# A four-layer graph attention kernel: mask gathers moved between layers, and the first edge blocks of layer 0 rearranged

## The chip, the core and the metric

The kernel runs on one core of a Trainium2 chip. The metric is the device time of one execution in microseconds. The core's engines are TensorE (PE, its weight loads PEld), VectorE (DVE), ScalarE (ACT), GpSimd (POOL) and SyncE (SP); indirect DMAs (gathers by a list of indices) are issued on POOL, most plain DMAs on SP. All waits between engines are semaphores placed by a tile framework from the program order: each engine executes its own instructions in the order in which the program issues them.

## What is computed

4096 nodes with 256 features each, an adjacency matrix of 4096 x 4096 int32, and four graph attention layers, each followed by a residual and a layer norm. Node degrees fall off along the index (the chance of an edge goes with the square root of 1/(i+1) and 1/(j+1)), so the matrix is dense in its first rows and columns and sparse elsewhere.

```python
def attention(logits, mask, h):            # in every layer, per head
    return softmax(where(mask, logits, -big), axis=1) @ h
# layer 0, 8 heads: leaky_relu(e_l[i] + e_r[j], 0.2) + gate * sum_f |c[i,f] - c[j,f]| * Wc[h,f]
# layer 1, 1 head:  s_src[i] + s_dst[j] + b_att,       h = x @ W_fc + b_fc
# layer 2, 4 heads: leaky_relu(s_row[i] + s_col[j], 0.2), elu, + x @ Wr + br, a layer norm of its own
# layer 3: h = x @ W0, then three attention layers (leaky_relu slope 0.01), each with elu
x = layernorm(x + layer0(x, adj)); x = layernorm(x + layer1(x, adj))
x = layernorm(x + layer2(x, adj)); x = layernorm(x + layer3(x, adj))
```

## The kernel before

**Two forms of sparsity.** Rows of the output are taken in 32 chunks of 128 in layer 0, and in 16 pairs of chunks (256 rows) in layers 1 to 3. Layer 0's chunk 0 is dense (`rows0`). Its other 31 chunks walk *edges*: for each row chunk a list of its edges is built, cut into 445 tiles of 128 edges and grouped in 64 blocks of 5 to 10 tiles. Layers 1 to 3 walk *nodes*: for each pair a list of the nodes with any edge into its 256 rows, in tiles of 128 nodes (`PAIR_TILES`: 32 tiles for pair 0, which is always dense, then 25, 22, 20, 19, 18, 17, 16, 16, 15, 15, 14, 14, 14, 13, 13, in all 251 for pairs 1 to 15). `DENSE = {1: 6, 2: 1, 3: 3}` says how many of the first pairs each later layer takes densely instead, all 32 node tiles with masks of their own: six in layer 1, so that layer 1 uses listed tiles of pairs 6 to 15 only (147), layer 2 those of pairs 1 to 15 (251), layer 3 those of pairs 3 to 15, three times. `sequence` interleaves a layer's dense and listed tiles; `LEAD[2] = 32` dense tiles go first in layer 2.

**Layer 0's start.** A projection of 32 node tiles fills V; every fourth tile the list builder `list_edges` is driven by six steps on DVE and ACT (L1153). Then V is multiplied by v tile by tile on DVE (L1175), and each tile is written to a table in DRAM (`table0`, L1177) on SP, 32 DMAs of 139 KB. `rows_by_edges` begins with constants: a memset of two `dT` tiles (L619), an iota on POOL (L707) and its casts to `number`, `count` and `place`.

**A block of edges** (`Block`, L621 to L702) goes through stages: `middle` (ACT: u), `spread` (DVE: of_row, then PE), `nodes` (DVE: the indices of the edges' nodes), `gather` (POOL: one indirect DMA from table0 for each tile, L659, into `g`, three buffers), `differences` (DVE: d, L666, PE, ACT), `pair_terms`, `weights`, `rows`, `values` (DVE multiplies g by w) and `add` (PE, L702, the last reader of g). The main loop is a software pipeline written out by hand: at block i it issues `spread` and `nodes` of block i+3, `gather` of block i+2, `differences` of block i+1, and the rest of block i. Between these steps `lane` lets other work run: the list builders of later chunks and of the pairs (DVE, ACT, PE), and two queues of mask jobs, one entry of each per edge tile.

**Mask jobs.** For each listed node tile of a pair the 128 x 256 adjacency cells are gathered by `listed_mask`: an indirect DMA on POOL into `pair_m` (L1020), a conversion to bytes on DVE (`pair_mb`, L1024) and a store to `listed_d` on SP (L1025). `job` issues the gather at once and the conversion seven entries later. `list_pair` puts the jobs of pairs 1 to 12 (`q < LATE`, 211 tiles) in the queue served in layer 0, those of pairs 13 to 15 (40) in `late_jobs`; `cell` is the tile of their indices. What is in the queue when the blocks end is drained there.

**Layers 1 to 3** run `attend` (L1266): for each tile of the sequence it issues the weights (for listed tiles a load of the mask on SP and an indirect gather of the node's row from the layer's table on POOL, L1312, 16 buffers; then DVE), the products of an earlier tile on PE, one step of `aside`, and one step of the ends of finished pairs (`one`: normalisation, the next layer's projection). In layer 1 `aside` is `late_masks()`: it issues one gather of `late_jobs` per tile and the conversion of the one five before. Layer 1 scales and writes its table on DVE and POOL first; in layer 2 ACT scales V and POOL issues four DMAs to table 2 (L1489); POOL also adds beta to the residual rows in `one` (L1527).

Of the kernel before, what the change touches and what calls it, by code (L numbers as in the profile page):

```python
# [49 lines left out]
F32 = mybir.dt.float32  # L50
# [3 lines left out]
U16 = mybir.dt.uint16  # L54
# [7 lines left out]
P = 128  # L62
# [11 lines left out]
DENSE = {1: 6, 2: 1, 3: 3}  # L74

LATE = 13
LEAD = {1: 80, 2: 32, 3: 44}
# [3 lines left out]
def gnn_stack(ctx: ExitStack, tc: tile.TileContext, a: dict, out: bass.AP):  # L81
# [365 lines left out]

    def rows0(chunks, ends, ps, ps_s, ps_acc):

        with ExitStack() as st:
            two = st.enter_context(tc.tile_pool(name="l0_all_two", bufs=2))
            three = st.enter_context(tc.tile_pool(name="l0_all_three", bufs=2))
            got = st.enter_context(tc.tile_pool(name="l0_all_got", bufs=3 * JR))
            cjs = []
# [142 lines left out]

    def rows_by_edges(prepared, pair_w, ends, ps, lane, first):  # L600

# [7 lines left out]
        with ExitStack() as st:  # L609
            two = st.enter_context(tc.tile_pool(name="l0_two", bufs=2))  # L610
            got = st.enter_context(tc.tile_pool(name="l0_got", bufs=3))
            ps_acc = st.enter_context(tc.tile_pool(name="l0_acc", bufs=2, space=PSUM))
            ps_x = st.enter_context(tc.tile_pool(name="l0_x", bufs=2, space=PSUM))
            number = two.tile([P, BT, P], U16, name="number", bufs=1)
            place = two.tile([P, max(EDGE_TILES)], F32, name="place", bufs=1)
            count = two.tile([P, P], F32, name="count", bufs=1)
            dTs = [two.tile([ROW1 + 1, P], F32, name=f"dT{k}", bufs=1) for k in range(2)]
            for d in dTs:
                nc.vector.memset(d[0:ROW1], 0.0)  # L619
                nc.vector.memset(d[ROW1:], 1.0)  # L620

# [81 lines left out]

            number_i = two.tile([P, BT * P], I32, name="number_i", tag="to_row")
            nc.gpsimd.iota(number_i, pattern=[[1, BT * P]], base=0, channel_multiplier=0)  # L707
            nc.vector.tensor_copy(number.rearrange("p t r -> p (t r)"), number_i)
            nc.vector.tensor_copy(count, number_i[:, 1:P + 1])
            place_i = two.tile([P, max(EDGE_TILES)], I32, name="place_i", bufs=1)  # L710
            nc.gpsimd.iota(place_i, pattern=[[P, max(EDGE_TILES)]], base=1, channel_multiplier=1)
            nc.vector.tensor_copy(place, place_i)

            plan = [Block(c, b, t0, n) for c in range(FIRST, NC) for b, (t0, n) in enumerate(blocks_of(c))]
# [5 lines left out]
            def at(i, *what):  # L720
                if 0 <= i < B:
                    for w in what:
                        getattr(plan[i], w)()

            dense = first(lambda shape, name: ps_x.tile(shape, F32, name=name, tag="x"),
                          lambda shape, name: ps_acc.tile(shape, F32, name=name, tag="acc0", bufs=1))
            given = 0
            for i in range(3):
                at(i, "middle", "spread", "nodes")
                if i < 2:  # L730
                    at(i, "gather")
            at(3, "middle")
            at(0, "differences", "pair_terms", "rows", "weights")
            late = []
            for i, blk in enumerate(plan):
# [7 lines left out]
                blk.values()  # L743
                at(i + 2, "gather")
                at(i + 1, "pair_terms")
                lane(share, c)
                at(i + 3, "nodes")
                lane(share, c)
# [21 lines left out]
    def layer0(proj):  # L770
        lin = 1.0 - 0.2
        with ExitStack() as st:
# [56 lines left out]
            nc.vector.memset(ones8, 1.0)  # L829
            near_by = [lp.tile([P, N + 8 * max(sum(k) for k in kinds)], BF16, name="near"), None]  # L830

            adj_pool = st.enter_context(tc.tile_pool(name="l0_adj", bufs=1))
# [140 lines left out]
            def list_pair(q):  # L973
# [3 lines left out]
                at = ats[q // BP]  # L977
                cell = lists.tile([P, A], I32, name="cell", bufs=LATE - 1) if q < LATE else keep.tile([P, A], I32, name=f"cell{q}")
                rhs = lists.tile([P, NT, 2, A], BF16, name="rhs", bufs=1)
# [30 lines left out]
                nc.vector.tensor_scalar(cell, x[:, 1], float(N // PW), float(q), ALU.mult, ALU.add)  # L1010
                if q < LATE:
                    jobs.extend([lambda i=i: listed_mask(at_pool, q, i, cell) for i in range(A)])
                else:
                    late_jobs.extend([lambda pool, i=i: listed_mask(pool, q, i, cell) for i in range(A)])
# [104 lines left out]
            with ExitStack() as pr:  # L1119
# [19 lines left out]
                for T in range(NT):  # L1139
# [13 lines left out]
                    if T % 4 == 3:  # L1153
                        for _ in range(6):
                            next(edge_lists)
# [4 lines left out]
                with tc.tile_pool(name="l0_st", bufs=1) as sp:  # L1160
# [13 lines left out]
                    for T in range(NT):  # L1174
                        nc.vector.tensor_tensor(by_head[:, T], by_head[:, T],  # L1175
                                                v[:, T, :].unsqueeze(2).to_broadcast([P, H0, D0 + 1]), ALU.mult)
                        nc.sync.dma_start(table0[T * P:(T + 1) * P, :], V[:, T, :])  # L1177

# [39 lines left out]
            def lane_e(n, c):  # L1218

                for _ in range(n):  # L1220
                    lane(1, (14 / EDGE_TILES[c], 5 / EDGE_TILES[c]))
                    ends.step()

            rows_by_edges(prepared, pair_w, ends, ps, lane_e,
                          lambda ps_s, ps_acc: rows0(FIRST, ends, ps, ps_s, ps_acc))
            proj.sums()
# [120 lines left out]
    def ends_of(ended, pairs, nxt, ps, one):  # L1347

        for _ in range(6):
            yield  # L1350
        if nxt is not None:
            yield from nxt.prepare(ps)
        for n in range(pairs):
            while not ended:
                yield
            yield from one(ended.pop(0), n)
# [7 lines left out]
    def layer1(proj, nxt, seq):  # L1364
        with ExitStack() as st:
# [50 lines left out]

            def late_masks():

                begun = []
                while late_jobs:  # L1420
                    begun.append(late_jobs.pop(0)(work))
                    if len(begun) > 4:
                        begun.pop(0)()
                    yield
                for convert in begun:
                    convert()

            def one(state, n):
# [15 lines left out]

            attend(seq, opened, weights, products, lambda ended: ends_of(ended, NP, nxt, ps, one), aside=late_masks())
            nxt.sums()
# [6 lines left out]
    def layer2(proj, V, nxt, seq):  # L1453
# [3 lines left out]
        with ExitStack() as st:  # L1457
# [54 lines left out]
            def products(some):  # L1512
# [4 lines left out]
                for (_, _, _, den, _), k, (g, w), last in some:  # L1517
                    for h in range(H2):
                        nc.tensor.matmul(den[32 * h:32 * h + 1, :], g[:, (h + 1) * (D2 + 1) - 1:(h + 1) * (D2 + 1)], w[:, h],  # L1519
                                         start=False, stop=last)  # L1520

            def one(state, n):
                q, _, num, den, _ = state
# [35 lines left out]

            attend(seq, opened, weights, products, lambda ended: ends_of(ended, NP, nxt, ps, one), rate=1.6, batch=2)  # L1560
            nxt.sums()
# [78 lines left out]
    def layers(p1, sparse):  # L1640

        def plan(n):
            k = DENSE[n] if sparse else NP
            return sequence(range(k), range(k, NP), LEAD[n])

# [28 lines left out]
    with tc.If(nc.values_load(over[0:1, 0:1], min_val=0, max_val=1) > 0):  # L1674
        with ExitStack() as st:
# [10 lines left out]
            for _ in rows0(NC, ends, ps, lambda shape, name: pool.tile(shape, F32, name=name, tag="s"),  # L1686
                           lambda shape, name: pool.tile(shape, F32, name=name, tag="acc0")):
                ends.step()
# [56 lines left out]
```

## Time and profile before

| | us |
|---|---|
| runs of the kernel before: median (lowest to highest) of 3 | 3169.53 (3165.16 to 3173.18) |
| the profiled execution: its time | 3159.55 |
| its span, first to last instruction | 3157.8 |
| mean granted TensorE clock in it | 0.881 of full speed |
| busy PE, PEld | 2574.0 (82%), 1798.6 (57%) |
| busy DVE, ACT, POOL | 2277.2 (72%), 1329.2 (42%), 1966.0 (62%) |
| layer 0: V multiplied from; table written; first gather | 104.6; 105.2 to 121.7; 135.3 |
| layer 0: gather 278 of 445; last gather | 747.0; 1149.7 |
| layer 1: first attention matmul | 1205.5 |
| layer 2: first weights; last tile | 1487.1; 2177.7 |
| layer 3: from; to the end | 2216; 3157.8 |

The page is taken from one execution of the program by the hardware profiler. Engines are busy when they execute an instruction; for POOL's indirect DMAs that is the time in which it makes their descriptors, not the time of the transfer. "Releaser" of an idle time is what ended it, inferred from semaphores. "issue" is time in which an engine waited for nothing that the profile shows. L12 is line 12 of the kernel before; a name such as g<-table says what an instruction writes and reads.

### The profile page before, as it was taken

The page shows a single profiled execution, that of the slowest core. Times are in us where ns is not written, and L with a number is a line of the kernel's source. Part 1 is how long each engine was busy: PE and PEld are TensorE (multiplying, and loading weights), DVE is VectorE, ACT ScalarE, POOL GpSimd, SP SyncE. Part 2 cuts the span into 40 slices and gives each one's busy share as a digit, 9 for nine tenths or more (in the row PEclk, how much of TensorE's full clock was granted, in tenths as well). Part 3 has the DMA queues.
Part 4 walks back from the last instruction along what each step waited for, and adds up shares of the span by engine and source line. Part 5 has one row for each costly group of instructions (what it writes and reads, how often), then busy time and mean ns, then how long its engine had stood idle before and what let it go on. Part 6 is the DMA issues. An engine that isn't in the chain of part 4 may idle for free.

```text
span 3157.8 us, 53737 instructions
## 1 busy us (share of the span) xinstructions
PE 2574.0 (82%) x16067; PEld 1798.6 (57%) x16067; DVE 2277.2 (72%) x7545; ACT 1329.2 (42%) x3895; POOL 1966.0 (62%) x1874
## 2 busy tenths in 40 slices
PE   6266666656666556998999999998899999999997
PEld 5154454444545445996233333333788878887875
DVE  6767888888888856776878788886565556556666
ACT  3365565646666434776212223333222322233334
POOL 0277667777777756772475566551477647755775
PEclk8587777777676778998999999999999999999999
DMA  6567786657666447675333333331544454446554
GB/s 183 164 195 224 234 249 190 206 169 220 198 217 204 115 128 233 200 206 155 105 89 101 96 104 99 100 86 51 171 137 135 114 174 135 135 113 183 166 164 129
DMA packets 345937, 495.65 MB, mean 157 GB/s; under 512 B 120476, under 2 KB 252418, under 8 KB 345634
## 3 DMA queue, kind: packets, MB, share of 16 engines
q0 software_dynamic: 87600, 252.16, 28.5%
q1 hardware_dynamic: 239608, 223.19, 23.6%
q10 hardware_dynamic: 18432, 16.79, 1.6%
q8 instruction: 132, 2.16, 0.3%
q14 instruction: 165, 1.35, 0.1%
HBM read 426.20 MB, written 65.72 MB: 156 GB/s over the span
## 4 chain that ended last, share of the span: by engine, by line
PE 51%; DMA 4%; DVE 2%; ACT 2%; issue 1%; POOL 0%; ACTq 0%; DVEq 0%; SPq 0%; POOLq 0%
PE acc L1605 20%; PE num L1515 12%; PE den L1519 8%; PE acc L1414 4%; PE ph L209 4%; DMA g<-table,pair_idx 3%; PE xT_p L198 1%; PE pr L213 1%; DVE w L1599 1%; PE pt L1537 0%; ACT V L1585 0%; POOL g L1312 0%; DVE y L1617 0%; DVE bn_st L305 0%; DVE y L314 0%
## 5 line engine op out<-in xcount | busy, mean ns | idle before, releaser
L1312 POOL DMA_INDIRECT g<-table,pair_idx x1010 | 1113.5, 1102 | 523.4 <-PE den L1519 102.6
L659 POOL DMA_INDIRECT g<-table,idx x445 | 515.5, 1158 | 194.0 <-issue 116.5
L1605 PE MATMUL acc<-g,w 128*128 128x257 f32 x2448 | 574.7, 382 | 17.3 <-DVE w L1599 16.7
L1605 PEld LDWEIGHTS acc<-g,w 128*128 128x128 f32 x2448 | 457.9, 190 | 94.7 <-DVE w L1599 30.0
L1506 DVE SCALAR_TENSOR_TENSOR w<-R,g,mask 128x256 f32<-128x256 f32 x1004 | 438.4, 486 | 48.2 <-PE den L1519 47.9
L1599 DVE SCALAR_TENSOR_TENSOR w<-R,g,mask 128x256 f32<-128x256 f32 x612 | 292.2, 482 | 244.8 <-PE acc L1605 172.8
L1515 PE MATMUL num<-w,g 128*64 128x256 f32 x2008 | 367.6, 395 | 0.0
L1020 POOL DMA_INDIRECT pair_m<-in_adjT,cell x251 | 279.2, 1112 | 112.4 <-issue 46.0
L702 PE MATMUL acc<-g,to_row 128*128 128x264 f32 x890 | 304.4, 502 | 41.3 <-DVE g L689 32.5
L1605 PE MATMUL acc<-V,w 128*128 128x257 f32 x1152 | 284.6, 387 | 16.1 <-ACT V L1585 9.1
L702 PEld LDWEIGHTS acc<-g,to_row 128*128 128x128 f32 x890 | 216.1, 255 | 95.1 <-DVE g L689 38.7
L1519 PE MATMUL den<-w,g 128*1 128x256 f32 x2008 | 266.5, 378 | 0.0
L1515 PEld LDWEIGHTS num<-w,g 128*64 128x64 f32 x2008 | 140.5, 135 | 196.9 <-DVE w L1506 97.4
L1605 PEld LDWEIGHTS acc<-V,w 128*128 128x128 f32 x1152 | 221.4, 194 | 49.7 <-ACT V L1585 15.0
L1615 ACT ACTIVATE y<-acc,inverse 128x256 f32<-128x256 f32 x96 | 44.7, 466 | 417.2 <-DVE inverse L320 365.9
L209 PE MATMUL ph<-wx,xT 128*128 128x258 f32 (+3 forms) x640 | 185.4, 423 | 33.4 <-ACT xT L200 19.7
L1599 DVE SCALAR_TENSOR_TENSOR w<-R,V,mask 128x256 f32<-128x256 f32 x288 | 137.0, 481 | 87.0 <-PE acc L1605 74.2
L905 DVE FIND_INDEX8 cand<-ones,near 128x8 uint16<-128x520 bf16 (+8 forms) x424 | 195.1, 469 | 0.0
L696 ACT ACTIVATE to_row<-count,side 128x128 f32<-128x128 f32 x445 | 145.4, 391 | 102.8 <-PE acc L702 99.5
L200 ACT ACTIVATE xT<-xT_p 128x128 f32<-128x128 f32 x320 | 86.0, 276 | 196.3 <-PE xT_p L198 187.2
L874 ACT ACTIVATE near<-ai 128x64 bf16<-128x64 int32 (+1 forms) x186 | 138.4, 765 | 59.4 <-DMA ai<-in_adj 31.2
L209 PEld LDWEIGHTS ph<-wx,xT 128*128 128x128 f32 x640 | 125.7, 206 | 64.8 <-ACT xT L200 31.4
(327 smaller groups left out, 4290.2 us busy)
## 6 DMA issues: line engine op xcount, KB each, us to landing
ai<-in_adj SPq DMA_DIRECT2D x124, 512.0 KB
mask<-listed_d SPq DMA_DIRECT2D x228, 128.0 KB
at<-in_adjT SPq DMA_DIRECT2D x96, 256.0 KB
mask<-mask_d SPq DMA_DIRECT2D x128, 128.0 KB
g<-table,pair_idx POOLq DMA_INDIRECT x1010
R<-r_d SPq DMA_DIRECT2D x56, 256.0 KB
table<-V POOLq DMA_DIRECT2D x12, 1032.0 KB
s<-y ACTq DMA_DIRECT2D x96, 128.0 KB
```

Of the source, the lines that this page charges most:

```text
L209: nc.tensor.matmul(ph, xT[:, kt, :], self.wx[:, kt, :], start=kt == 0, stop=kt == 1)
L659: nc.gpsimd.indirect_dma_start(self.g[:, t, :], None, table0[:, :], bass.IndirectOffsetOnAxis(ap=self.idx[:, t:t + 1], axis=0))
L696: nc.scalar.activation(self.to_row[:, t], count, AF.Abs, bias=self.side[:, t, 0:1])
L702: nc.tensor.matmul(acc, self.to_row[:, t], self.g[:, t, 0:VW], start=self.t0 + t == 0, stop=last and t == n - 1)
L905: nc.vector.max_index(cand[:, s], ones8, near[:, at:at + W])
L1020: nc.gpsimd.indirect_dma_start(m[:, :], None, pair_cells, bass.IndirectOffsetOnAxis(ap=cell[:, k:k + 1], axis=0))
L1312: nc.gpsimd.indirect_dma_start(g[:, :], None, self.table[:, :], bass.IndirectOffsetOnAxis(ap=pair_idx[:, at:at + 1], axis=0))
L1506: nc.vector.scalar_tensor_tensor(w[:, h], R[:, h].rearrange("p t i -> p (t i)"), g[:, VW2 + h:VW2 + h + 1], m, ALU.max, ALU.mult)
L1515: nc.tensor.matmul(num[h % 2 * D2:(h % 2 + 1) * D2, h // 2, :], g[:, h * (D2 + 1):h * (D2 + 1) + D2], w[:, h], start=False, stop=last and ...
L1519: nc.tensor.matmul(den[32 * h:32 * h + 1, :], g[:, (h + 1) * (D2 + 1) - 1:(h + 1) * (D2 + 1)], w[:, h], start=False, stop=last)
L1599: nc.vector.scalar_tensor_tensor(w, R[:, q * PW:(q + 1) * PW], g[:, C + 1:C + 2], m, ALU.max, ALU.mult)
L1605: nc.tensor.matmul(t, w[:, it * P:(it + 1) * P], g[:, 0:C + 1], start=k == 0, stop=last)
```

## The change

1. *Where the masks are gathered.* Pairs 6 to 15 (147 tiles) are gathered in layer 0, the pairs that layer 1 needs; pairs 1 to 5 (104 tiles) go to `late_jobs`, and `late_masks` moves from layer 1 to layer 2, as its `aside`. In layer 2 the listed pairs are taken in the order 6 to 15, then 1 to 5.
2. *The gather buffers of layer 0.* `g` has four buffers, not three, and the gather of block i+3 is issued right after its `nodes`, where that of block i+2 came before, one stage earlier in the loop.
3. *The constants.* The iota, the casts and the memsets of `dT` move from the head of `rows_by_edges` to the head of layer 0.
4. *The dense rows.* `rows0` opens its pools in a scope of layer 0 and returns a generator; its PSUM banks come through a dictionary that `rows_by_edges` fills.
5. *The list builder's head start.* Four steps every fourth projection tile, not six.
6. *The table.* Every fourth tile of the multiplication goes to POOL, and four tiles are written by one DMA.

In the order in which the engines execute it, the 147 mask gathers of layer 0 stand between the last 167 of the 445 row gathers, about one to one; 33 of layer 2's 104 mask gathers stand before its four table writes, the other 71 among the next 66 row gathers. Before, layer 0's masks began behind row gather 81, and its last 45 row gathers had none between them.

```diff
-LATE = 13
-            got = st.enter_context(tc.tile_pool(name="l0_got", bufs=3))
+            got = st.enter_context(tc.tile_pool(name="l0_got", bufs=4))
-            number_i = two.tile([P, BT * P], I32, name="number_i", tag="to_row")
...
-            dense = first(lambda shape, name: ps_x.tile(shape, F32, name=name, tag="x"),
-                          lambda shape, name: ps_acc.tile(shape, F32, name=name, tag="acc0", bufs=1))
+            banks.update(acc=ps_acc, x=ps_x)
+            dense = first
             for i in range(3):
-                at(i, "middle", "spread", "nodes")
-                if i < 2:
-                    at(i, "gather")
+                at(i, "middle", "spread", "nodes", "gather")
...
                 blk.values()
-                at(i + 2, "gather")
                 at(i + 1, "pair_terms")
                 lane(share, c)
-                at(i + 3, "nodes")
+                at(i + 3, "nodes", "gather")
...
+            number = lp.tile([P, BT, P], U16, name="number")
+            with tc.tile_pool(name="l0_iota", bufs=1) as ip:
+                number_i = ip.tile([P, BT * P], I32, name="number_i")
+                nc.gpsimd.iota(number_i, pattern=[[1, BT * P]], base=0, channel_multiplier=0)
...
-                cell = lists.tile([P, A], I32, name="cell", bufs=LATE - 1) if q < LATE else keep.tile([P, A], I32, name=f"cell{q}")
+                now = q >= DENSE[1]
+                cell = lists.tile([P, A], I32, name="cell", bufs=NP - DENSE[1]) if now else keep.tile([P, A], I32, name=f"cell{q}")
-                if q < LATE:
+                if now:
                     jobs.extend([lambda i=i: listed_mask(at_pool, q, i, cell) for i in range(A)])
                 else:
                     late_jobs.extend([lambda pool, i=i: listed_mask(pool, q, i, cell) for i in range(A)])
...
-                        for _ in range(6):
+                        for _ in range(4):
                             next(edge_lists)
...
                     for T in range(NT):
-                        nc.vector.tensor_tensor(by_head[:, T], by_head[:, T],
-                                                v[:, T, :].unsqueeze(2).to_broadcast([P, H0, D0 + 1]), ALU.mult)
-                        nc.sync.dma_start(table0[T * P:(T + 1) * P, :], V[:, T, :])
+                        (nc.gpsimd if T % 4 == 3 else nc.vector).tensor_tensor(
+                            by_head[:, T], by_head[:, T], v[:, T, :].unsqueeze(2).to_broadcast([P, H0, D0 + 1]), ALU.mult)
+                        if T % 4 == 3:
+                            nc.sync.dma_start(table0[(T - 3) * P:(T + 1) * P, :].rearrange("(t p) c -> p t c", p=P), V[:, T - 3:T + 1, :])
...
-            attend(seq, opened, weights, products, lambda ended: ends_of(ended, NP, nxt, ps, one), aside=late_masks())
+            attend(seq, opened, weights, products, lambda ended: ends_of(ended, NP, nxt, ps, one))
...
-            attend(..., rate=1.6, batch=2)
+            attend(..., rate=1.6, batch=2, aside=late_masks())
...
         def plan(n):
             k = DENSE[n] if sparse else NP
-            return sequence(range(k), range(k, NP), LEAD[n])
+            listed = list(range(k, NP))
+            if n == 2:
+                listed = [q for q in listed if q >= DENSE[1]] + [q for q in listed if q < DENSE[1]]
+            return sequence(range(k), listed, LEAD[n])
```

## The prediction

> **What bounds the kernel now.** Read in this order: span and clock (3157.8 us, 0.881, one core), the slices, the chain of waits, busy time by stretch, then waits and groups inside each stretch.
>
> ```profile
> PE   6266666656666556998999999998899999999997
> DVE  6767888888888856776878788886565556556666
> POOL 0277667777777756772475566551477647755775
> PE 51%; DMA 4%; DVE 2%; ACT 2%; issue 1%; POOL 0%; ACTq 0%; DVEq 0%; SPq 0%; POOLq 0%
> ```
>
> The chain is PE's in layers 1 to 3. The first 15 slices (79 us each, all layer 0) show nobody full, so layer 0 is cut at landmarks: 104.6 (V multiplied), 747 (gather 278 of 445), 1150 (last gather), 1205 (layer 1's first matmul). The columns are us, busy PE, PEld, DVE, ACT, POOL with counts, PE clock, DMA share, GB/s.
>
> ```profile
> 104.60:747.00 642.40, 391.70 (x3025) 300.62 (x3025) 506.21 (x1867) 361.80 (x976) 447.65 (x393) 0.73 0.72 211
> 747.00:1150.00 403.00, 252.69 (x2048) 194.53 (x2047) 338.73 (x1320) 230.52 (x618) 309.18 (x265) 0.72 0.60 180
> 1545.00:1745.00 200.00, 200.00 (x1371) 68.87 (x1370) 158.66 (x432) 44.05 (x123) 117.61 (x84) 1.00 0.33 92
> ```
>
> In the first two DVE (79%, 84%) and POOL (70%, 77%) share the work; the third, layer 2, is full PE. DVE's waits in 104.6 to 747 (total us, times, longest):
>
> ```profile
> DVE d L666 <- DMA g<-table,idx: 54.2, 13, 8.1
> DVE pair_mb L1024 <- DMA pair_m<-in_adjT,cell: 15.7, 5, 7.0
> DVE pair_mb L1024 <- issue: 10.1, 3, 5.0
> DVE d L666 <- DMA pair_m<-in_adjT,cell: 6.1, 3, 2.6
> DVE pair_mb L1024 <- DMA listed_d<-pair_mb: 4.7, 5, 2.6
> DVE d L666 <- issue: 4.3, 2, 3.3
> ```
>
> DVE waits for POOL's gathers: 95.1 us of its 136.2 idle. POOL's groups in 747 to 1150, then layer 2, then layer 3 (busy, mean ns, idle before and what ended it):
>
> ```profile
> L659 POOL DMA_INDIRECT g<-table,idx x168 | 200.6, 1194 | 58.3 <-issue 43.6 <-PE total_p L957 3.7 <-PE acc L702 3.6
> L1020 POOL DMA_INDIRECT pair_m<-in_adjT,cell x97 | 109.1, 1125 | 35.8 <-issue 14.3 <-DVE cell L1010 6.6 <-DVE cand L905 2.7
> ...
> L1312 POOL DMA_INDIRECT g<-table,pair_idx x251 | 357.8, 1425 | 249.6 <-PE den L1519 102.6 <-DVE w L1506 81.4 <-issue 20.7
> ...
> L1312 POOL DMA_INDIRECT g<-table,pair_idx x594 | 590.7, 994 | 208.1 <-DVE w L1599 75.3 <-PE acc L1605 62.0 <-issue 35.1
> ```
>
> From 747 on POOL sets the pace: most of its 94 us idle is 0.305 us of issue per gather. Each of its 265 gathers takes 403/265 = 1.521 us of the stretch.
>
> **Part 1, the start of layer 0.** DVE is 98% busy before the multiplication (24.0 of 24.6 us in 80 to 104.6). Sixteen list steps fewer stand ahead: 16 searches (0.368 + 0.076), 5 replacements, 6 maxima and small operations, 11.7 us by their rows. The multiplication starts at 92.9, and the 11.7 us come back on DVE later. Then the table:
>
> ```profile
> 105.15 16.56 SPq L1177 DMA_DIRECT2D table<-V  x32
> ...
> 126.20 0.17 DVE L619 MEMSET dT<- 64x128 f32 x1 [2.84 <-DMA g<-table]
> 126.62 1.19 POOL L707 IOTA number_i<- 128x1280 int32 x1 [118.37 <-DMA g<-table]
> 127.85 0.83 DVE L708 CAST number<-number_i 128x1280 uint16<-128x1280 int32 x1
> ```
>
> 32 x 139 KB go in 20.7 us at a DMA share near 1: the transfer binds, not the issue. Eight DMAs of four tiles save nothing I count; nor do the 24 multiplications left on DVE (24 x 0.346 = 8.3 us) with 8 on POOL, priced by its nearest row (128x256 add, 0.744 to 0.848 us), 6 to 7 us beside them. The table lands at 92.9 + 20.7 = 113.6. Everything before the first gather (135.27) still waits for it: DVE's next instruction reads back from the table, as `u` and `of_row` follow in program order. What goes is iota and casts, 2.1 of the 8.65 us.
>
> [...]
>
> **Part 2, layer 0 to gather 278.** All 114 masks in this stretch leave it (147 stay in layer 0, interleaved one to one with the last 167 gathers). POOL then needs 278 x 1.45 to 1.565 = 402 to 435 us and has slack; DVE binds. Its busy time: 506 less 26 (110 conversions of 0.304, of which some catch up), less 1.9 constants, less 2.8 multiplications, less 13 (the fourth buffer puts a gather a block earlier, 1/39 of 506 shifts past the landmark), plus 11.7 = 474. Idle: the 95 us of waits on gathers fall to a residue of 15 (bounds 0 and 95, nearest the low end, since gathers go out a block, 642/39 = 16 us, earlier and no mask stands in front); 41 others stay; 3 for a memset that now stands behind the table. So 59, and the stretch ends at 92.9 + 474 + 59 = 626, not 747.
>
> **Part 3, to the last gather.** 167 + 147 = 314 entries x 1.521 = 478 (1.447 to 1.565: 454 to 491), so 1104 instead of 1150; the same 55 us tail: layer 1 opens 47 us earlier. With part 2's idle between 44 and 139 the bounds are -86 and +46.
>
> **Part 4, layer 1.** Its 40 masks, half at the border (1180 to 1205, where POOL and SP issue them before the table): -3 (0 to -6). Later they lay beside PE (246 busy of 270).
>
> **Part 5, into layer 2.** 24 conversions stand on DVE ahead of layer 2's first weights (1487.1), each waiting for a gather that POOL may start when layer 1's memory is free, 1455: 1455 + 24 x 1.30 + 4 = 1490, so +3 (0 to +9). Behind them SP's mask loads wait. The 33 gathers ahead of POOL's four table writes end by 1500 while ACT still scales V for the last write (1512.8): hidden; without that cover they cost up to 33 x 1.3 = 43 us.
>
> **Part 6, inside layer 2.** 71 masks alternate with the next 66 row gathers, and 8 additions take 9 us. PE needs 633 us/251 = 2.52 a tile from 1545 to 2178, so 66 tiles last 166; gathers run 41 us ahead (gather 15 at 1543.7, its use 1584.8). POOL has 207 us for 137 entries. At layer 3's 0.994 + 0.305 = 1.30 it needs 187, nothing lost; at layer 2's own 1.425 + 0.305 = 1.73, 246, so +39; at the full row without waits for PE (357.8 + 249.6 - 102.6)/251 = 2.01, 285, +78. I take 1.52, between the first two, since layer 0's mixture with conversions ran so: 217, +10. The conversions (71 x 0.283 = 20 us) bring DVE from 158.7 to about 178 of 200: still beside PE. If PE starves, every `products` call waits, then the ends behind it. Pairs 1 to 5 come last, so each mask store lands some hundred us ahead of its load.
>
> A gather may be held by DVE:
>
> ```profile
> 1835.70 9.18 DVE L1506 SCALAR_TENSOR_TENSOR w<-R,g,mask 128x256 f32<-128x256 f32 x23
> 1837.92 7.78 POOL L1312 DMA_INDIRECT g<-table,pair_idx  x1 [3.31 <-DVE w L1506]
> ```
>
> The Trainium skill (SBUF — State Buffer, "Who interferes with whom") makes the pair of ports shared by DVE and GpSimd an exclusive lock, taken by tensor_scalar in its two-port modes too, though it infers that two-input operations spare descriptor generation. The row above speaks against that inference. If every conversion held POOL, an estimate by that rule is 20 us more in layer 2.
>
> **Sum.** -47 - 3 + 3 + 10 = -37. It is made on the profiled execution (span 3157.8, time 3159.55), 10 us below the median of the runs, 3169.53; the difference goes on the median: 3133.
>
> **Rivals.** (B) POOL sets all of layer 0. For it: from first to last gather 1014.9 us over 656 entries, 1.547 each, in both stretches alike. Then 592 x 1.547 = 916, -99, with the 13.8 us earlier start -113, with parts 4 to 6 -103: 3067. Against it: 95 us of DVE waiting for POOL come in bursts, and DVE's work hardly shrinks (850 to 839). (C) The gain is given back: stage one keeps idle as latencies of DVE, ACT and PE in each block replace the wait for POOL, and POOL still has 314 entries in a row behind it. All of it kept (136 for 59) would be -37 + 77 = +40; with masks gone from in front of the gathers half is likelier: +2, 3171, no change. For it: 41 us of idle not due to gathers; against: the longest waits are gathers. (D) POOL starves PE in layer 2. At 2.01 us an entry +78 replaces +10: 3169.5 - 47 + 78 = 3200, slower. It decides from (207 - 9 + 56)/137 = 1.85 us an entry, where the +56 eat the 47 and leave 9 over. For it: the held gather, and layer 2's row; against: gathers that find a free buffer ran at 1.25 us apart right after it. That preparation doesn't run beside the table, as named, is already in part 1.
>
> **Numbers.** Chances: mine 0.51, B 0.15, C 0.13, D 0.21. Mine alone spans 3095 to 3160 (part 2's idle 44 to 100, part 6's 0 to +39). The range reaches half into B and most of D: 3078 to 3192. Faster by over 0.3% (9.5 us, about what a measurement of this kernel tells from no change) is mine and B: 0.66; same C: 0.13; slower D: 0.21.
>
> **What would show it.** V multiplied at about 93, the first gather at 120; DVE's waits on g near 15 us up to gather 278, at 626 (B: 560; C: 700); POOL's 314 entries 1.5 us apart to 1104; layer 1 opening at 1158; first layer 2 weights 32 us after layer 1's last matmul plus 3; in layer 2, PE without gaps over masks 34 to 104, or with gaps before L1515's matmuls whose releaser is a gather or a `w` behind one (D). Wrong if the four-buffer gathers wait for `add` to release them, or if the masks' loads in layer 2 wait for their stores.

## The result, and the profile after

The changed kernel took 3149.3 us in the median of 4 runs (3144.37 to 3152.28), the kernel before, beside it, 3167.35: a ratio of 0.994 (95% interval 0.9917 to 0.9963), 18 us less. Six more runs on another chip gave 3145.15 against 3165.85, 0.9938 (0.9919 to 0.9958). The forecast was 3133, 36 us less than its base of 3169.53: right in sign and inside the range, and twice too large. The runs of this document fell on several chips, and on one of them every kernel took about 15% longer (the kernel before 3651 us in the median of 18 runs), so each run is held against the runs of the kernel before on its own chip. The profiled execution has a span of 3142.7 us and a clock of 0.884. Its lines, first the slices (78.6 us each) and the chain by engine:

```profile
PE   7377667666665458997999999998899999999987
DVE  6768899988987536776788888786565555556666
POOL 1366566567777724777677755663577557755775
PE 42%; DMA 3%; DVE 2%; ACT 1%; issue 1%; POOL 0%; SPq 0%; DVEq 0%; ACTq 0%; POOLq 0%
```

DVE shows a 9 in slices six to eight and eleven, where it had an 8 before, and the end of layer 0 (slices thirteen to fifteen) is emptier on it. Busy time by stretch (columns as in the prediction), with the same landmarks: V multiplied, gather 278, last gather; then layer 2, from its first weights to its last, and the same of the kernel before:

```profile
92.80:658.80 566.00, 379.15 (x2996) 285.15 (x2996) 475.40 (x1773) 354.97 (x970) 332.98 (x285) 0.78 0.69 206
658.80:1118.50 459.70, 269.70 (x2111) 203.44 (x2109) 359.72 (x1400) 241.36 (x641) 358.26 (x309) 0.68 0.59 177
...
1459.90:2168.60 708.70, 706.07 (x4736) 245.80 (x4736) 584.13 (x1633) 196.03 (x593) 492.97 (x360) 1.00 0.40 113
...
1487.10:2179.40 692.30, 691.71 (x4760) 245.45 (x4760) 566.17 (x1553) 199.11 (x604) 386.87 (x285) 1.00 0.34 97
```

Before, the first stretch lasted 642.4 us with DVE busy 506.2, now 566.0 with 475.4; the second lasted 403.0, now 459.7 with POOL busy 358 of it. DVE's waits in the first stretch (total us, times, longest), and POOL's groups in the second:

```profile
DVE d L661 <- DMA g<-table,idx: 45.8, 11, 6.8
DVE mb L400 <- DMA at<-in_adjT: 12.2, 15, 1.8
```

```profile
L654 POOL DMA_INDIRECT g<-table,idx x168 | 198.4, 1181 | 55.4 <-issue 50.1 <-DMA g<-table,idx 1.5 <-PE acc L697 1.1
L1023 POOL DMA_INDIRECT pair_m<-in_adjT,cell x141 | 160.8, 1140 | 46.3 <-issue 24.4 <-DVE cand L906 3.8 <-DVE pair_mb L1027 3.4
```

There is no mask in the first stretch any more, and so none of the 30.5 us that conversions waited there (15.7 + 10.1 + 4.7 before); the wait on g fell from 54.2 to 45.8 only. In the second stretch POOL waits for little but its own issue: 459.7/309 = 1.488 us for each entry, a gather of rows or of a mask (six of layer 0's 147 masks come behind its last row gather).

The landmarks of the profiled runs on chips on which the kernel before took some 3166 us, in us from the start of its trace, and then durations (layer 1: its first to its last attention matmul; into layer 2: from there to DVE's first weights of layer 2; layer 2: those to its last weights; the rest from there to the end):

| run | first gather | gather 278 | last gather | layer 1 opens | layer 1 | into layer 2 | layer 2 | rest | span |
|---|---|---|---|---|---|---|---|---|---|
| before | 135.3 | 747.0 | 1149.7 | 1205.5 | 250.0 | 31.6 | 692.3 | 978.4 | 3157.8 |
| changed | 119.6 | 658.8 | 1118.5 | 1177.6 | 243.4 | 38.9 | 708.7 | 974.1 | 3142.7 |
| changed, again | 116.4 | 660.1 | 1118.3 | 1177.3 | 242.6 | 38.4 | 706.5 | 974.0 | 3138.7 |
| parts 2 to 6 only | 116.1 | 757.1 | 1184.8 | 1241.1 | 249.8 | 32.2 | 692.1 | 977.2 | 3192.4 |
| three buffers | 119.5 | 671.9 | 1125.2 | 1178.0 | 243.6 | 37.3 | 708.4 | 973.9 | 3141.2 |
| 13 to 15 in layer 1 | 119.9 | 667.6 | 1084.3 | 1144.1 | 249.6 | 38.1 | 708.2 | 972.5 | 3112.5 |
| the same, later in layer 2 | 115.4 | 665.8 | 1088.0 | 1149.6 | 247.7 | 40.4 | 706.4 | 975.1 | 3119.2 |
| 1 and 2 in layer 0 | 119.3 | 725.1 | 1179.0 | 1239.5 | 244.1 | 37.4 | 695.7 | 973.6 | 3190.3 |
| 10 to 15 in layer 1 | 117.5 | 663.9 | 1063.2 | 1121.0 | 302.3 | 38.3 | 705.9 | 972.5 | 3140.0 |
| the same, ACT converts | 116.1 | 655.9 | 1057.1 | 1116.0 | 294.4 | 40.4 | 742.0 | 973.5 | 3166.3 |

In the changed kernel layer 0 gives 28 us and layer 1 seven; the way into layer 2 takes back 7 and layer 2 itself 16 (14 in the second execution); what follows gives 4.

### The profile page after: what moved, and what is told of

It is laid out like the page before. It is cut to its first block, busy times and chain, and to the rows that moved or that the text cites. A ratio compares the mean times of both kernels' runs of the same rounds, so it can differ in the third digit from the quotient of the medians.

```text
span 3142.7 us, 53738 instructions
## 1 busy us (share of the span) xinstructions
PE 2597.0 (83%) x16067; PEld 1797.3 (57%) x16067; DVE 2275.7 (72%) x7537; ACT 1326.2 (42%) x3895; POOL 2004.1 (64%) x1882
## 5 line engine op out<-in xcount | busy, mean ns | idle before, releaser
L654 POOL DMA_INDIRECT g<-table,idx x445 | 525.4, 1181 | 288.1 <-issue 171.8
L1023 POOL DMA_INDIRECT pair_m<-in_adjT,cell x251 | 307.1, 1223 | 91.6 <-issue 35.4
L697 PE MATMUL acc<-g,to_row 128*128 128x264 f32 x890 | 304.7, 502 | 39.9 <-DVE g L684 30.5
L1514 PE MATMUL den<-w,g 128*1 128x256 f32 x2008 | 276.0, 378 | 0.0
L691 ACT ACTIVATE to_row<-columns,side 128x128 f32<-128x128 f32 x445 | 146.7, 391 | 108.7 <-PE acc L697 104.4
```

The costliest lines, as they stand in the source:

```text
L654: nc.gpsimd.indirect_dma_start(self.g[:, t, :], None, table0[:, :], bass.IndirectOffsetOnAxis(ap=self.idx[:, t:t + 1], axis=0))
L691: nc.scalar.activation(self.to_row[:, t], count, AF.Abs, bias=self.side[:, t, 0:1])
L697: nc.tensor.matmul(acc, self.to_row[:, t], self.g[:, t, 0:VW], start=self.t0 + t == 0, stop=last and t == n - 1)
L1023: nc.gpsimd.indirect_dma_start(m[:, :], None, pair_cells, bass.IndirectOffsetOnAxis(ap=cell[:, k:k + 1], axis=0))
```

## The experiments

The first four ran on the chip of the 3651 us. The changed kernel was not run there, so its 0.994 doesn't stand beside them.

**The move of the masks alone.** Everything as before but for part 1.

```diff
-                if q < LATE:
+                now = q >= DENSE[1]
+                if now:
                     jobs.extend([lambda i=i: listed_mask(at_pool, q, i, cell) for i in range(A)])
...
@@ layer1
-            attend(..., aside=late_masks())
@@ layer2
+            attend(..., aside=late_masks())
```

> Part 1 of the change alone (the masks moved), everything else as before. Theory: the waits on g before 250 us have no mask in front of them and stay, as does the late start (first gather 135); POOL still has about 314 entries in a row at the end of layer 0, and layer 2 with its border pays some 23 us. So layer 0 ends at most 15 to 25 us earlier and the whole is about as before: ratio to before 0.998 to 1.004. Rival: the move of the masks is what made the kernel faster, ratio 0.993 to 0.996.

Measured: 3608.78 against 3651.3, ratio 0.9885 (0.9838 to 0.9933). The theory falls, the rival holds and more (on this chip; the masks alone were not run on another): gather 278 came at 727 and the last one at 1274, where parts 2 to 6 alone (next, same chip) had 844 and 1363.

**Parts 2 to 6 alone.** Run on both kinds of chip.

```diff
-                now = q >= DENSE[1]
-                if now:
+                if q < LATE:
...
@@ layer1
+            attend(..., aside=late_masks())
@@ layer2
-            attend(..., aside=late_masks())
...
@@ plan
-            return sequence(range(k), listed, LEAD[n])
+            return sequence(range(k), range(k, NP), LEAD[n])
```

> Parts 2 to 6 of the change without part 1: pairs 1 to 12 gathered in layer 0, 13 to 15 in layer 1, layer 2 as before. Theory: the start is 15.7 us earlier, POOL keeps the same 656 entries to the border at about 1.53 us, so layer 0 ends 12 to 25 us earlier and layers 1 and 2 last as long as before (250, 31, 693): ratio 0.992 to 0.996, as good as the whole change. Rival: with masks in front of the gathers the earlier start is only waited away, ratio 0.998 to 1.000.

Measured: 3662.74 against 3651.3, ratio 1.0026 (0.9992 to 1.0059), above the theory and near the rival. And again, on a chip like the first:

> Parts 2 to 6 without the move of the masks, once more, since in the first four runs every kernel took 15% longer. Theory after those: with masks in front of the gathers the earlier start and the fourth buffer are waited away, and the move of the masks makes the gain: ratio 0.996 to 1.001, first gather at 117 to 120 but gather 278 at 725 to 750. Rival: the start's 16 us stay: ratio 0.992 to 0.995.

Measured: 3197.28 against 3166.5, ratio 1.0102 (1.0083 to 1.0121), slower by 31 us and above both ranges. The first gather is 19 us earlier than before, gather 278 at 757 ten us later, and layer 1 opens 36 us later. Busy time by stretch of the second run, and DVE's waits in 120 to 750:

```profile
92.80:757.10 664.30, 398.86 (x2996) 301.40 (x2997) 497.39 (x1869) 358.42 (x967) 438.92 (x386) 0.73 0.67 202
757.10:1184.80 427.70, 273.08 (x2112) 205.23 (x2110) 353.46 (x1372) 238.17 (x636) 322.50 (x275) 0.69 0.60 179
```

```profile
DVE d L662 <- DMA g<-table,idx: 55.1, 14, 7.3
DVE pair_mb L1027 <- DMA pair_m<-in_adjT,cell: 44.5, 12, 10.1
```

DVE works no longer (497 against 506 before) and waits more: 44.5 us at conversions for their masks, where the kernel before had 15.7 in the row of that name. POOL stood here, in the same execution, while DVE did this:

```profile
408.51 0.94 POOL L655 DMA_INDIRECT g<-table,idx  x1 [0.30 <-issue]
447.06 0.94 POOL L655 DMA_INDIRECT g<-table,idx  x1 [37.60 <-PE acc L698]
```

```profile
404.26 0.44 DVE L401 TENSOR_SCALAR mb<-at 128x512 uint8<-128x512 int32 x1 [3.29 <-DMA at<-in_adjT]
406.33 0.43 DVE L401 TENSOR_SCALAR mb<-at 128x512 uint8<-128x512 int32 x1 [1.63 <-DMA at<-in_adjT]
409.54 0.43 DVE L401 TENSOR_SCALAR mb<-at 128x512 uint8<-128x512 int32 x1 [2.78 <-DMA mask_d<-mb]
```

POOL waits 37.6 us for the `add` that frees a gather buffer, while DVE, whose work that `add` needs, meets waits of 2 to 3 us for loads and stores of the dense masks one after the other; the longest wait for a buffer before was 9.4, in the changed kernel 10.0. A wait of 36 to 38 us stands in the three traces in which parts 2 to 6 meet the masks of pairs 1 and 2 in layer 0 (both of these, and the run with pairs 1 and 2 below), and in no other. With the masks of pairs 1 to 12 among the gathers, then, parts 2 to 6 cost 31 us where the theory of the first of these runs had 12 to 25 of gain. Which of them does it (the earlier gather, the 16 list steps fewer) was not tried apart.

**Three gather buffers**, and the gather of block i+2 in its old place.

```diff
-            got = st.enter_context(tc.tile_pool(name="l0_got", bufs=4))
+            got = st.enter_context(tc.tile_pool(name="l0_got", bufs=3))
...
+                at(i + 2, "gather")
...
-                at(i + 3, "nodes", "gather")
+                at(i + 3, "nodes")
```

> The change with three gather buffers and the gather of block i+2 in its old place. Theory: without masks in the stretch to gather 278, POOL has slack, and DVE's waits on g stay near 46 to 60 us, all but some before 250 us; gather 278 at 659 to 670, ratio 0.994 to 0.997. Rival: the fourth buffer is what removed the waits after 250 us; then they come back, 90 us in all, gather 278 near 700, ratio 0.999 to 1.004.

Measured: 3590.59, ratio 0.9834 (0.9791 to 0.9877), below both ranges, which were worked out from traces of faster chips. It lets parts 2 to 6 be priced on one chip, but for the fourth buffer: by themselves they cost 11 us (3662.74 for 3651.3), on top of the masks they gain 18 (3590.59 for 3608.78; the intervals overlap). Again, on the other kind of chip:

> The changed kernel with three gather buffers and the old place of the gather, once more. Theory: no mask stands in front of gathers 1 to 278, so the buffer matters little: waits on g 45 to 65 us, gather 278 at 659 to 675, ratio to before 0.993 to 0.998. Rival: the buffer and the earlier gather carry the gain of this stretch: gather 278 at 690 to 720, ratio 1.000 to 1.010.

Measured: 3141.64 against 3166.5, ratio 0.9925 (0.99 to 0.9949), no different from the changed kernel's 0.9938. Gather 278 comes 12 us later and POOL makes it up behind it. The theory holds, though its ratio lies a hair below the range: with the masks nearly all behind gather 278, the fourth buffer and the earlier gather are worth nothing that the times show (DVE's waits up to gather 278, then the two stretches):

```profile
DVE d L661 <- DMA g<-table,idx: 46.9, 11, 7.3
```

```profile
92.80:671.90 579.10, 388.96 (x3059) 293.66 (x3058) 482.57 (x1799) 362.50 (x989) 340.80 (x289) 0.77 0.68 205
671.90:1125.20 453.30, 264.32 (x2053) 199.23 (x2053) 354.78 (x1387) 234.38 (x630) 352.06 (x308) 0.68 0.60 177
```

**Layer 2's masks begun behind its dense tiles.**

```diff
                 begun = []
+                for _ in range(LEAD[2]):
+                    yield
                 while late_jobs:
```

> The change with layer 2's mask gathers begun only after its 32 dense tiles, behind the four table writes on POOL. Theory: the 33 gathers ahead of the table writes cost layer 2 its start: one of them lay held for 36.5 us beside DVE's dense tiles and the writes came at 1500, 40 us after layer 2's first weights; behind the writes, first gather about 33 us after the first weights (58 in the change), border 31 and not 39 us, layer 2 695 to 700 and not 709: ratio 0.987 to 0.991. Rival: the 104 gathers and conversions beside the listed tiles cost it, wherever they begin: ratio 0.993 to 0.996.

Measured: 3612.6, ratio 0.9903 (0.9867 to 0.9939). The edit did only half of what it was to do: the framework still issued 32 mask gathers ahead of the four table writes, and only the later ones stand further back (114 row gathers before the last mask, not 82). Layer 2 took 771 us, and 754 and 763 in the three-buffer run and the first run of the same chip. So nothing is gained by beginning later. What was to be told apart is told below.

**The changed kernel again, and pairs 13 to 15 back in layer 1.** Four runs on one chip, the first of them the changed kernel.

> The changed kernel again, beside the next three on their chip. On the chip of the first four runs every kernel took longer (before 3651); there the change was not run. If a chip like the first is met, ratio 0.992 to 0.996; if one like that of the four, 0.982 to 0.990, since POOL's entries took 1.90 us there and the change takes 64 of them out of layer 0.

Measured: 3145.15, 0.9938, as above.

```diff
-                now = q >= DENSE[1]
+                now = DENSE[1] <= q < 13
...
-                    late_jobs.extend([lambda pool, i=i: listed_mask(pool, q, i, cell) for i in range(A)])
+                    (late_jobs if q < 13 else tail_jobs).extend([lambda pool, i=i: listed_mask(pool, q, i, cell) for i in range(A)])
...
@@ layer1
+            attend(..., aside=late_masks())
```

(`late_masks` of layer 1 goes through `tail_jobs`.)

> The change with the masks of pairs 13 to 15 (40 tiles) gathered in layer 1, as before the change: 107 in layer 0, 40 in layer 1, 104 in layer 2. Theory: layer 0 ends on POOL (314 entries in a row from gather 278 on, 46 of 58 us busy in the last stretch while DVE is busy 23), so 40 entries fewer at 1.46 us end it 40 to 58 us earlier, and layer 1 gets back some 7: ratio to the changed kernel 0.985 to 0.991. Rival: list building on DVE sets the end of layer 0, or layer 1 pays the same again: ratio to the changed kernel 0.997 to 1.003.

Measured: 3120.16, ratio to before 0.9855 (0.9834 to 0.9875), to the changed kernel 3120.16/3145.15 = 0.992. This is the fastest version of all. POOL has 274 entries behind gather 278:

```profile
667.60:1084.30 416.70, 264.36 (x2080) 199.23 (x2079) 349.71 (x1363) 238.15 (x636) 317.78 (x275) 0.71 0.61 183
...
1144.10:1393.70 249.60, 232.87 (x1635) 219.04 (x1636) 178.05 (x658) 167.48 (x556) 168.68 (x172) 0.97 0.72 205
```

416.7/274 = 1.52 us an entry: layer 1 opens 33 us earlier (40 to 58 were expected, so the theory's size was too large) and takes 7 longer. The sign is the theory's, the ratio lies just outside both ranges.

**The same, with layer 2's masks begun later.**

```diff
                 begun = []
+                for _ in range(LEAD[2]):
+                    yield
                 while late_jobs:
```

> As the kernel before it, and layer 2's mask gathers begun behind its 32 dense tiles. Theory: the border into layer 2 shortens by 3 to 8 us, the listed part pays 10 to 20 for gathers that then all stand beside listed tiles: 0 to +12 us against the run before it. Rival: gathers ahead of the table writes cost more than gathers beside listed tiles: -10 to -20.

Measured: 3121.7, ratio 0.9857 (0.9834 to 0.988), +1.5 us against the one before it, inside the theory's 0 to +12. But neither of its two parts came: the way into layer 2 lasts 40.4 us and not 38.1, layer 2 706.4 and not 708.2, and here too 32 gathers stayed ahead of the table writes. What differs is worth a look. In five traces (both of the changed kernel, three buffers, 13 to 15 in layer 1, 1 and 2 in layer 0) one mask gather was held there for 32.6 to 36.5 us; first the changed kernel's POOL, then its DVE at the same time:

```profile
1462.30 36.52 POOL L1023 DMA_INDIRECT pair_m<-in_adjT,cell  x1 [0.30 <-DVE w L1501]
...
1517.31 1.00 POOL L1318 DMA_INDIRECT g<-table,pair_idx  x1 [13.62 <-DMA table<-V]
```

```profile
1459.90 39.68 DVE L1501 SCALAR_TENSOR_TENSOR w<-R,V,mask 128x256 f32<-128x256 f32 x100 [2.31 <-ACT V L1482]
```

One gather lasts nearly as long as DVE's unbroken run of 100 operations; the four table writes behind it come at 1500, and the first row gather 57.4 us after layer 2's first weights (31.9 before). In the later version no mask gather of layer 2 lasted over 1.6 us, and the first row gather came 27.1 us after the first weights. It was held itself, beside the rest of the same run of DVE:

```profile
1464.72 11.90 POOL L1318 DMA_INDIRECT g<-table,pair_idx  x1 [5.51 <-DMA table<-V]
...
1437.65 39.77 DVE L1512 SCALAR_TENSOR_TENSOR w<-R,V,mask 128x256 f32<-128x256 f32 x100 [5.41 <-ACT V L1493]
```

And yet the way into layer 2 and layer 2 together took 746.8 us against 746.3. The 32 dense tiles (some 81 us of PE, at the prediction's 2.52 each) cover the 25 to 29 us.

**Pairs 1 and 2 in layer 0 as well**, 57 masks left for layer 2.

```diff
-                now = q >= DENSE[1]
+                now = q >= DENSE[1] or q <= 2
```

> The change with the masks of pairs 1 and 2 (47 tiles) gathered in layer 0 as well, where their lists come first, beside gathers before number 278; 57 left for layer 2. Theory: POOL's 160 us of gaps there take the gathers, DVE pays 47 x 0.30 = 14 us at most, and layer 2 with its border loses 10 to 14 us of its 24: -5 to +5 us against the changed kernel. Rival: masks in front of gathers bring DVE's waits back, +25 to +45 us.

Measured: 3191.16, ratio 1.0077 (1.0058 to 1.0095), +46 us against the changed kernel: the rival, to the upper end of its numbers and over. Gather 278 comes 65 us later for 47 gathers, 1.4 us for each, although POOL was busy in only 333 of the 566 us of this stretch without them; and the long wait for a buffer is here too (POOL's timeline, DVE's waits up to gather 278, layer 2's busy time).

```profile
450.86 0.94 POOL L654 DMA_INDIRECT g<-table,idx  x1 [37.09 <-PE acc L697]
```

```profile
DVE d L661 <- DMA g<-table,idx: 54.8, 12, 8.0
DVE pair_mb L1027 <- DMA pair_m<-in_adjT,cell: 20.3, 5, 8.8
```

```profile
1521.00:2216.70 695.70, 692.68 (x4736) 244.66 (x4736) 573.33 (x1586) 197.12 (x598) 460.94 (x314) 0.99 0.37 104
```

Layer 2, with 57 masks for 104, lasts 695.7 and not 706.5: within 3.4 us of before. It has the new order of the pairs too, so that order costs no more than this.

**Pairs 10 to 15 in layer 1** (83 tiles).

```diff
-                now = DENSE[1] <= q < 13
+                now = DENSE[1] <= q < 10
...
-                    (late_jobs if q < 13 else tail_jobs).extend(...)
+                    (late_jobs if q < 10 else tail_jobs).extend(...)
```

> The change with the masks of pairs 10 to 15 (83 tiles) gathered in layer 1; 64 in layer 0, 104 in layer 2. Theory: with 40 moved so, layer 1 opened 33 us earlier and took 6.5 us more; 43 more open it 15 to 33 us earlier again (DVE, 360 us busy of 417 behind gather 278, sets the lower end) and cost layer 1 another 4 to 12: ratio to before 0.977 to 0.983. Rival: layer 0's end is set by DVE and the lists by now, ratio 0.984 to 0.988.

Measured: 3142.02 against 3166.5, ratio 0.9928 (0.991 to 0.9946), above both ranges. Layer 0 does what the theory says (layer 1 opens 23 us earlier than with 13 to 15 there), and layer 1 takes 302 us, not 254 to 262:

```profile
663.90:1063.20 399.30, 262.16 (x2111) 199.41 (x2109) 343.02 (x1328) 239.41 (x640) 267.63 (x231) 0.72 0.58 174
...
1121.00:1423.30 302.30, 253.64 (x1635) 235.26 (x1636) 187.50 (x701) 168.22 (x556) 210.39 (x215) 0.89 0.68 193
```

```profile
L1318 POOL DMA_INDIRECT g<-table,pair_idx x147 | 146.0, 993 | 44.8 <-issue 13.1 <-DVE w L1409 7.9 <-DVE Vg L1387 4.0
L1023 POOL DMA_INDIRECT pair_m<-in_adjT,cell x60 | 58.6, 976 | 21.1 <-issue 9.1 <-DVE pair_mb L1027 5.3 <-DVE w L1409 2.7
```

Most idle time in POOL's rows is the 0.30 us of issue before each gather: 0.99 + 0.30 = 1.29 for each entry. In the versions above, on chips of this kind, layer 1's 147 row gathers stand back to back, some 195 us from the first to the last (147 x 1.29 = 190); here they take 248. Of 40 masks 38 go ahead of them, while the table is built, and 2 among them; of 83, 38 ahead and 45 among them. The 43 more among them are 43 x 1.29 = 55 us, and the layer takes 53 longer. The theory had taken PE for its bound, which is busy in 233 of 250 us, but POOL feeds it at about the same pace.

**ACT converts**, in all layers.

```diff
-                    nc.vector.tensor_scalar(mb, m, 0.0, None, ALU.is_gt)
+                    nc.scalar.copy(mb, m)
```

> As the kernel before it, with all 251 conversions of masks on ACT and not on DVE. Theory: layer 2's loss of 15 us is DVE's (98% busy while the conversions stand between its weights, PE's matmuls waiting for w one by one), so on ACT layer 2 lasts 693 to 698 and not 708: ratio 0.972 to 0.979. Rival: the loss is POOL's gathers or the order of the pairs, then layer 2 stays at 705 to 711 and the ratio within 0.002 of the run before it.

Measured: 3176.3, ratio 1.0032 (1.0018 to 1.0045), +34 us against the run before it. Both theories miss: layer 2 takes 742 us. ACT's waits at the border (1397 to 1500), then PE's in 1449 to 1620:

```profile
ACT pair_mb L1027 <- DMA pair_m<-in_adjT,cell: 20.8, 8, 7.9
ACT pair_mb L1027 <- DMA listed_d<-pair_mb: 10.7, 7, 5.3
```

```profile
PE pt L1554 <- ACT sb L1546: 18.4, 2, 12.2
PE ph L207 <- ACT xT L198: 8.5, 1, 8.5
```

ACT stands at conversions for 31 us, V's scaling and then the ends of pairs come behind them, and PE waits for these. The first row gather came 45 us after the first weights, not 29. So it doesn't tell DVE from POOL as the price of the masks in layer 2. The rows of the changed kernel's second execution point to POOL, in 1548 to 1728, where the masks and row gathers alternate (POOL's groups, then DVE's waits):

```profile
L1023 POOL DMA_INDIRECT pair_m<-in_adjT,cell x65 | 68.7, 1058 | 19.2 <-DVE w L1501 9.2 <-issue 3.4 <-DVE inverse L320 0.9
L1318 POOL DMA_INDIRECT g<-table,pair_idx x65 | 67.8, 1043 | 19.2 <-issue 11.0 <-PE den L1514 3.0 <-DMA pair_m<-in_adjT,cell 1.5
L1533 POOL TENSOR_TENSOR xr<-xr,beta 128x256 f32<-128x256 f32 x8 | 6.7, 842 | 0.2
```

```profile
DVE pair_mb L1027 <- issue: 18.9, 10, 3.6
DVE pair_mb L1027 <- DMA pair_m<-in_adjT,cell: 9.3, 7, 2.6
```

POOL's busy time and its 0.30 us of issue per entry fill the 180 us (143.2 + 38.6); DVE is the one that waits. 65 listed tiles last 180/65 = 2.77 us each, and 2.52 without masks: 16 us, near the 14 to 16 that layer 2 lost. This is read from the rows; no run changed POOL's share alone. PE's row can't tell: it is busy in 706.1 of layer 2's 708.7 us, as it was in 691.7 of 692.3 before; the profile models the ends of matmuls.

## Why the prediction was right in sign and twice too large

Of the 22 us between the forecast's -37 and the -15 of the two profiled spans, 19 lie in layer 0, in parts 1 to 3 of the prediction (the numbers in brackets below are the prediction's, not those of the list of changes).

- *The start (part 1).* Multiplication from 92.8 (predicted 92.9), first gather at 119.6 (120). From the first multiplication to SP's next transfer behind the table 19.5 us pass, for the 20.7 of the sum; when the table has landed the trace does not show. Right in itself. But an earlier start is not a gain by itself: parts 2 to 6 of the change, without the masks' move, start as early and are 31 us slower than before. The start and the masks were taken as independent terms, and they are not. The sum has no figure for parts 2 to 6 alone; the 13.8 us that rival B gives the earlier start would leave some 23 of the 37 to the masks. Measured, the masks' move on top of the others is worth 3197.28 - 3145.15 = 52 us (two chips, with 3166.5 and 3165.85 for the kernel before), and the others by themselves cost 31. That the sum came out with the right sign is in part luck: these two errors have opposite signs.
- *Gather 278 at 626 (part 2).* Measured 659 and 660. DVE's busy time was right: 475.4 for 474. Its idle time was 90.6, not 59, and the term that failed is the residue of 15 for waits on g: 45.8. Of these, 40 lie before 240 us, at the first blocks, and the trace of before has 32.7 there too; its first mask gather comes at 268 (DVE's waits in 104.6 to 268 before, then in 92.8 to 240 after):

```profile
DVE d L666 <- DMA g<-table,idx: 32.7, 8, 5.8
...
DVE d L661 <- DMA g<-table,idx: 40.0, 9, 6.8
```

  No mask was ahead of them, so moving masks could not remove them, and their earlier gathers did not. A look at when the waits lay, not only at their sum, would have shown it. It is 31 of the 33 us by which this stretch ended later than predicted. One of the prediction's signs of being wrong came: the four-buffer gathers do wait for `add` (POOL's waits up to gather 278, before and after):

```profile
POOL g L659 <- PE acc L702: 32.3, 12, 9.4
...
POOL g L654 <- PE acc L697: 69.6, 17, 10.0
```

  It cost little, since POOL had slack: behind 240 us DVE waited 5.8 us on g.
- *The last gather at 1104 (part 3).* 1118.5. POOL sets this stretch, as said, at 1.488 us an entry for 1.521, and with 309 entries (gather 278 counted) for 314, since six masks came behind the last row gather; 460 us for 478 gives 18 of the 33 back. Layer 1 opened 28 us earlier, not 47.
- *Layer 1 (part 4).* -6.6 for -3, just outside its bounds of 0 to -6.
- *Into layer 2 (part 5).* +7 for +3, inside its bounds of 0 to 9. The 24 conversions stand where they were said to; the variants with mask gathers there all show 37 to 40 us, those without 32. That the table writes stay hidden was right in the end for another reason than the one given: the first row gather behind them was 25 us late, and the dense tiles covered it.
- *Inside layer 2 (part 6).* +16 and +14 for +10. From the first row gather to the last mask POOL took 215.7 us; 217 was worked out, but by luck, from the wrong pair of numbers: 153 entries stood in it (71 masks and 82 row gathers, not 66), at 1.41 us with the eight additions, and not 1.52. That conversions hold POOL, as the rule of the Trainium skill on the shared pair (SBUF — State Buffer, "Who interferes with whom") would allow, is hardly seen: 1.04 to 1.06 us for a gather beside them, 0.99 in layer 1. What the prediction says of a gather held by DVE's `w` is seen, and more often than its one row lets expect (last section).
- *The rivals.* B (POOL sets all of layer 0) is refuted: DVE was 84% busy and POOL 59% up to gather 278. DVE's busy time in the two stretches went from 844.9 to 835.1 us, where B's text has 850 to 839. C named the right place, idle of DVE that stays, and about the right share, 32 of 77 us, but another reason: what stayed are waits for gathers, and the idle for other reasons went from 41 to 45 us only. D did not come: at 1.41 us an entry the price stayed far from 1.85.
- Layer 3 lasts 4 us less in all versions with the new order of pairs; that was not looked into.

## What to carry to other kernels

A wait summed over a stretch says nothing about what the change removes: look when each of them happened, and whether the thing to be moved was there yet. Work taken off one queue (64 gathers off POOL in layer 0) is priced where it leaves and where it lands, and the landing has an edge: layer 1 took 40 masks for 7 us and 83 for 59, because its row gathers stand back to back and only 38 masks fit ahead of them. Two parts of a change whose instructions pass through the same buffers and the same queue are not to be added up; run each without the other.

## What was not expected of the hardware

- A gather of 0.95 us lasted 36.5 us beside 100 DVE operations without a pause between them (39.68 us), each with two operands in SBUF. Held gathers are no exception: in layer 2 of the kernel before 16 row gathers lasted over 3 us, each beside such a run of `w`, the longest 12.37 us (POOL, then DVE at the same time):

```profile
1598.52 12.37 POOL L1312 DMA_INDIRECT g<-table,pair_idx  x1 [0.30 <-DVE w L1506]
...
1594.54 15.52 DVE L1506 SCALAR_TENSOR_TENSOR w<-R,g,mask 128x256 f32<-128x256 f32 x39
```

  In layer 3, where DVE waits for PE between the same operations, none lasted over 2.2 us. Some gathers pass inside a run (the one ahead of the 36.5 us took 0.99), and why is open. The Trainium skill (SBUF — State Buffer, "Who interferes with whom") infers, for `tensor_tensor`, that a two-input operation leaves descriptor generation alone, while it does collide with a GpSimd instruction that reads SBUF. These gathers, which take their indices from SBUF, are held, so the inference does not carry over to them.
- The same kernel (parts 2 to 6) took 3192.4 us on one chip and 3661.6 on the other in its profiled executions. DVE and POOL were busy alike (2278.7 and 2270.1 us, 1974.8 and 1957.0), PE a little longer (2597.9 and 2722.0, at granted clocks of 0.877 and 0.838), but layer 1 took 330.5 us and not 249.8. The slower trace has waits that nothing in it ends ("remote", 61.5 us in one row of DVE's), and the other has none. What slows that chip is open.
